# A stack of four modulated convolutions on one core: the last product in one piece, input transforms of the last quads in another order, and the last edge product seven turns later

## The chip, the core and the metric

The program runs on one core of a Trainium2 chip. The time is the device time of one execution in microseconds (us), and the span is the part of it from the first to the last profiled instruction. The engines are TensorE (PE, with its weight loads as PEld), VectorE (DVE), ScalarE (ACT), GpSimd (POOL) and SyncE (SP, which here only issues transfers). Each has its own queue of instructions and takes them strictly in order.

## The reference

The input `x` is 128 samples of 64 channels by 1024 points. Four layers of three taps are applied, and the result is added to `x`:

```python
def _layer(x, style, w, b, mw, mb, typ):
    s = style @ mw.T + mb
    weight = SCALE * w * s[:, None, :, None]
    demod = lax.rsqrt(jnp.sum(weight * weight, axis=(2, 3)) + EPS)
    weight = weight * demod[:, :, None, None]
    # 'same': 3 taps; 'upsample': transposed, step 2, then blur;
    # 'downsample': blur, then 3 taps with step 2
    ...
for i, typ in enumerate(('same', 'upsample', 'same', 'downsample')):
    out = _layer(out, style, weights[i], biases[i], mod_w[i], mod_b[i], typ)
x = x + out
```

Each sample has its own weights, since `style` differs per sample. All is float32.

## The kernel before, in words

The four layers are linear in `x` once the weights of a sample are known. So the kernel multiplies the four weight sets of a sample together, with the blurs, into one filter of nine taps (`Wf`), the residual being one more addend, and then runs this filter over `x`. The three outer points at either end of a row do not obey that filter; a separate small chain of products computes corrections for them.

Four samples make a **quad**: two lie on the two halves of the 128 partitions, and two stand side by side (index `c` or `s`, 0 and 1). There are 32 quads (`NQ`), numbered 0 to 31, and each is loaded as three planes of 344 columns (every third point).

The nine taps over three planes are done with five products instead of nine, each of three taps. Their inputs are sums and differences of planes made ahead: `T3` (`in3`), `G` (`in_g01`, `in_g2`), then from `G` the tiles `T12` (`in1`, `in2`, mostly on GpSimd) and `T04` (`in04`, on VectorE). `in04(q, pairs)` can be done for both pairs of samples at once or for one pair (`PAIR[0]`, `PAIR[1]`). There is one `G` buffer, and there are two `T04` buffers. The products are `conv3`, `conv1`, `conv2`, `conv4`, `conv0`: `conv4` and `conv0` read `T04`, `conv4` into the PSUM tile `Y`, the others into the quad's own pair of banks `psA`. Between products VectorE and ScalarE take intermediate sums (`copy_m3`, `sum1`, `sum2`), since the banks go on accumulating. `sum2` writes into `Y` what `conv4` then adds to.

The main loop is a software pipeline in an order written out by hand (no scheduler reorders it): `turn_of(q)` finishes quad q, runs the first products of quad n = q+1, makes the filter of quad c = q+2 and begins that of quad q+4. Turns 4 to 28 are such turns; after them comes a hand-written stretch for q = 29 and one for quads 30 and 31.

What the steps of the prediction touch:

- `product`, L807, issues the 12 matmuls of one product (each counts twice in the profile). In the last stretch the last product (`conv0` of quad 31) is made in two rounds: first the outer 88 columns at either side (`SIDES`), then the 166 in the middle (`MIDDLE`); after each, ScalarE turns bank 0 and VectorE bank 1 into the plane of `o` (`output`, L891), and each piece has its own store, on the ScalarE and the SyncE queue. `o` is one tile `o1` for both rounds.
- `SLOTS`, L1303: at the top of turn q, if q-1 is a key, one group of edge products is put on TensorE into the banks of quad q-1. The last group is `ends3`; `rest3` then reads it into the table of corrections `Oe`.
- `gather(q)` brings the edge points of quad q into `Oc`: for quads below `LATER_ENDS` as plain copies on ScalarE, for the later ones as a subtraction of `Oe` on GpSimd, one turn later. `correct_all` subtracts `Oe` from all the copies at once on VectorE and stores them; the rest are stored at the very end (`store_ends`).

Of the kernel before, what the change touches and what calls it, by code (L numbers as in the profile page):

```python
# [55 lines left out]
K = 3  # L56
# [7 lines left out]
def kernel(  # L64
# [9 lines left out]
    nc = tc.nc  # L74
    NP, P, NXC = x.shape
    B = 2 * NP
    NQ = B // 4
# [5 lines left out]
    nc_v, nc_a, nc_g = nc.vector, nc.scalar, nc.gpsimd  # L83
# [91 lines left out]
    NB = 342  # L175
    Y = ps_y.tile([P, 2, 512], F32, name="Y")
# [428 lines left out]
    def tap(kind, g):  # L605
        return range(9)[TAPS[kind]][g]
# [132 lines left out]
    Ts = {}  # L739
# [3 lines left out]
    BOTH_PAIRS = slice(0, 2)  # L743
    PAIR = slice(0, 1), slice(1, 2)
# [43 lines left out]
    def in04(q, pairs=BOTH_PAIRS):  # L788
        if q < NQ:
            t, g = t_tile(q, "T04"), Gs[q]  # L790
            a, b = g[:, pairs, :NJ], g[:, pairs, 2 * PL : 2 * PL + NJ]
            both = lambda v, step: bass.AP(
                v.tensor, v.offset, [*(list(d) for d in v.ap[:-1]), [step, 2], [1, NJ]]
            )
            nc_v.tensor_sub(t[:, pairs, :, :NJ], both(a, PL), both(b, 1))  # L795

    WHOLE = slice(0, NB)
    SIDES, MIDDLE = 88, slice(88, NB - 88)

    def columns(v, at):  # L800

        if at != SIDES:
            return v[..., at]
        ap = [list(d) for d in v.ap]
        return bass.AP(v.tensor, v.offset, [*ap[:-1], [ap[-1][0] * (NB - SIDES), 2], [ap[-1][0], SIDES]])

    def product(q, m, ps, groups=range(K), alone=False, at=WHOLE):  # L807

        W, H_ = Wq[q]
        tag, i = SLOT[m]  # L810
        for g in groups:
            for s, rows in enumerate(HALF):
                for c, cols in enumerate(HALF):
                    if m in (0, 4):
                        w = W[rows, tap(m // 2, g), c, :]
                    else:
                        w = H_[rows, m - 1, g, c, :]
                    nc.tensor.matmul(  # L818
                        columns(ps[s][cols], at),
                        w,  # L820
                        columns(Ts[q, tag][rows, c, i, g:], at),
                        start=(g == 0 and (m == 3 or alone)),
                        stop=(g == K - 1),
                        skip_group_check=True,
                    )
# [4 lines left out]
    m3c, y1w = {}, {}  # L830
# [7 lines left out]
    def banks(q):  # L838
        return A[q] if isinstance(A[q], list) else [A[q][:, s] for s in range(2)]
# [31 lines left out]
    def sum2(q, steps=(0, 1)):  # L871
        if 0 in steps:
            m3 = m3c.pop(q)
            for s, a in enumerate(banks(q)):
                sum_of(Y[:, s, :NB], m3[:, s], 3.0, a[:, :NB])
        for s, a in parts(q) if 1 in steps else ():
            nc_v.tensor_sub(y1w[q][:, s], y1w[q][:, s], a)

    def conv4(q, *groups):
        product(q, 4, Y_banks, groups or range(K))  # L880

    def conv0(q, *groups):
        product(q, 0, banks(q), groups)

    NO = NB + 2
    o_tiles = [const.tile([P, 2, K, NO], F32, name=f"o{i}") for i in range(2)]
    for t in o_tiles:
        nc_g.memset(t[:, :, :, NB:], 0.0)
    os = [t[:, :, :, :NB] for t in o_tiles] * (NQ // 2)

    def output(q, i, s, eng=nc_a, at=WHOLE):  # L891

        d3, add = td[:, q, s : s + 1], tb[:, q, s : s + 1]
        src = columns((banks(q)[s], y1w[q][:, s], Y[:, s])[i], at)
        dst = columns(os[q][:, s, i], at)
        if eng is nc_a:
            nc_a.activation(dst, src, AF.Identity, bias=add, scale=d3)  # L897
        else:
            eng.tensor_scalar(dst, src, d3, add, op0=ALU.mult, op1=ALU.add)  # L899

    def store(q, s, planes=slice(0, K), queue=nc.sync):
        queue.dma_start(
            out[q, :, s, planes.start * NO : planes.stop * NO],
            o_tiles[q % 2][:, s, planes].rearrange("c i j -> c (i j)"),
        )
# [262 lines left out]
    def edges(q, planes):  # L1168
        o = os[q].rearrange("c r i j -> c r j i")
        at, step = ((0, NB - 1), (0, NB - 2))[planes.start > 0]  # L1170
        return o[:, :, at : step + 1 : step, planes], 2 * q

    LATER_ENDS = NQ - 6

    def correct(q, planes, eng=nc_g):
        src, b = edges(q, planes)
        at = slice(b, b + 2)
        if eng is nc_a:
            eng.copy(Oc[:, at, :, planes], src)
        else:  # L1180
            eng.tensor_sub(Oc[:, at, :, planes], src, Oe[:, at, :, planes])  # L1181

    def gather(q):
        for planes in (slice(1, K), slice(0, 1)):
            correct(q, planes, nc_a if q < LATER_ENDS else nc_g)

    def correct_all(n):
        nc_v.tensor_sub(Oc[:, : 2 * n], Oc[:, : 2 * n], Oe[:, : 2 * n])
        store_ends(0, n)

    def store_ends(i, j, queue=nc.sync):
        at = slice(12 * i, 12 * j)
        queue.dma_start(out_ends[:, at], Oc.rearrange("c b e j -> c (b e j)")[:, at])
# [5 lines left out]
    BOTH = nc_a, nc_v  # L1199
# [100 lines left out]


    REST = PART[2]
    SLOTS = {9: (ends0, rest0), 10: (ends1, rest1), 12: (ends2, rest2), 16: (ends3, rest3)}  # L1303

    def high(n):
        return Y[:, 1, NB + 4 : NB + 4 + n]
# [44 lines left out]
    def last_factors():  # L1351
# [22 lines left out]
        14: lambda: (blur_side(0, 0), blur_side(1, 0)),  # L1374
        15: lambda: (blur_side(0, 1), blur_side(1, 1)),
        16: lambda: (blur_side(0, 2), blur_side(1, 2)),
        NQ - 5: lambda: correct_all(LATER_ENDS),
    }

    def extra(*at):  # L1380
# [2 lines left out]
    def side(work, q):  # L1383
        work.get(q, lambda: None)()
# [118 lines left out]
    def turn_of(q):  # L1503
        n, c, s = q + 1, q + 2, q + 4
        entry = q == FIRST
        stage2(c)
        if entry:
            sum2(q)
            conv4(q)
            combine_a(n)  # L1510
            r_sums(c, nc_v)
        else:
            if q - 1 in SLOTS:
                SLOTS[q - 1][0](banks(q - 1))
            conv2(q)
            r_sums(c, nc_g)
            if q - 1 in SLOTS:
                SLOTS[q - 1][1](A[q - 1])
            sum2(q)
            in2(n, nc_g)  # L1520
        side(TABLES, q)
        for i in range(3):
            load(c + 1, slice(i, i + 1))
        stage3_b(c, open_a(n))
        if entry:
            conv0(q, 0, 1)
        else:
            combine_a(n)
            conv4(q)
        stage3_a(c)  # L1530
        combine_b(n)
        conv3(n)
        if entry:
            copy_m3(n)
            stage1_a(s)
        outputs(q, 2)
        if not entry:
            if s < NQ:
                stage1_a(s)
            copy_m3(n)  # L1540
        in04(n)
        if sharing(q):
            share_sums(c + 1)
        in_g2(c)
        side(SIDE, q)
        if q in SMALL:
            l, bs = SMALL[q]
            nc_v.memset(high(bs.stop - bs.start), 0.0)
        conv0(q, *((2,) if entry else range(K)))
        if entry:  # L1550
            conv1(n, 0, 1)
        outputs(q, 1)
        if s < NQ:
            stage1_b(s)
        in_g01(c)
        if sharing(q):
            share(c + 1, banks(q))
            share_copy(c + 1)
        outputs(q, 0)
        if q < LATER_ENDS:  # L1560
            gather(q)
        conv1(n, *((2,) if entry else range(K)))
        if q in SMALL:
            small(q)
        sum1(n)
        in3(c)
        if q > LATER_ENDS:
            gather(q - 1)
        if s == NQ:
            in04(c, PAIR[0])  # L1570
        in1(c, nc_g)
        if s + 1 < NQ:
            scale3(s + 1)
# [6 lines left out]
    q, n, c = NQ - 3, NQ - 2, NQ - 1  # L1580
# [10 lines left out]
    outputs(q, 2)  # L1591
    copy_m3(n)
    in3(c)
    in04(n, PAIR[1])
    in_g01(c)
    stage3(c, 1)
    conv0(q, 0)
# [18 lines left out]
    q, n = NQ - 2, NQ - 1  # L1616
# [44 lines left out]
        plus(i, o[:, i, 2], Y_banks, one_td, m3[:, i])  # L1661
        store(q, i, slice(2, K))
    correct(q, slice(1, K), nc_v)
    for at in (SIDES, MIDDLE):
        product(q, 0, banks(q), at=at)
        for i, (eng, queue) in enumerate(zip(BOTH, (nc_a, nc.sync))):
            output(q, 0, i, eng, at)
            queue.dma_start(
                columns(out[q, :, i, :NO], at), columns(o_tiles[q % 2][:, i, 0], at)
            )  # L1670
        if at == SIDES:
            correct(q, slice(0, 1), nc_v)
            store_ends(LATER_ENDS, NQ)


# [74 lines left out]
```

## Time and profile before

| what | value |
|---|---|
| median of three runs | 477.81 us (477.81, 476.05, 477.82) |
| the profiled execution | 474.59 us |
| its span | 472.8 us |
| TensorE busy | 466.1 us, 99% of the span |
| VectorE, ScalarE, GpSimd busy | 414.7, 318.7, 176.8 us |
| mean granted TensorE clock | 0.999 |
| written to and read from memory | 34.01 and 35.03 MB, 146 GB/s over the span |

A busy TensorE is not one at its peak: matmuls are pipelined and their ends are modelled. A row of the timeline has start, duration, engine, line, operation, output and inputs, count, and in brackets how long the engine had been idle and who released it. `T` in it is `T3`, `T12` or `T04`, by the line: L764 is `in3`, L781 `in1`, L786 `in2`, L795 `in04`. L715 is a helper of many sums.

### The profile page before, as it was taken

Reading aid. Unit: us, or ns where it says so; the run is one execution under the profiler, and the core shown is the slowest. Engines: PE = TensorE matmul, PEld = TensorE weight load, DVE = VectorE, ACT = ScalarE, POOL = GpSimd, SP = SyncE. Lnnn points to the kernel's source line nnn. Section 1 sums busy time; section 2 is a strip of 40 time slices with the busy share of each in tenths; the row PEclk is TensorE's granted clock in tenths of the full one; section 3 lists DMA queues with packets and bytes.
Section 4 is the critical chain, followed back from the end, with each engine's and each line's share of the span. In section 5 each row is a group of like instructions: output and inputs, shape, how many; then the busy total and the mean of one; then the engine's idle time right before and its main releaser. Section 6 shows DMA issues by size and latency. Waiting matters only on the chain. (4 is left out here: it accounts for less than half of the span.)

```text
span 472.8 us, 27015 instructions
## 1 busy us (share of the span) xinstructions
PE 466.1 (99%) x12052; PEld 341.6 (72%) x12052; DVE 414.7 (88%) x678; ACT 318.7 (67%) x764; POOL 176.8 (37%) x216
## 2 busy tenths in 40 slices
PE   9999999999999999999999999999999999999995
PEld 8887778777767777767876677776677777777753
DVE  5899989778989999998899988889888888998994
ACT  5566676677766667765777757777766777776463
POOL 3634141763448542233332234432233442333310
PEclk9999999999999999999999999999999999999999
DMA  6326554554445553444544445544455554445224
GB/s 179 94 93 209 170 153 153 153 166 141 150 139 167 154 181 113 144 143 155 167 147 144 150 151 158 183 143 146 140 153 162 175 175 132 151 148 170 92 84 162
DMA packets 53380, 70.79 MB, mean 150 GB/s; under 512 B 6672, under 2 KB 51472, under 8 KB 53264
## 3 DMA queue, kind: packets, MB, share of 16 engines
q1 hardware_dynamic: 52768, 68.84, 46.0%
q8 instruction: 94, 1.54, 1.4%
q10 hardware_dynamic: 496, 0.22, 0.2%
q14 instruction: 22, 0.18, 0.1%
HBM read 35.03 MB, written 34.01 MB: 146 GB/s over the span
## 5 line engine op out<-in xcount | busy, mean ns | idle before, releaser
L818 PE MATMUL psA<-T,H 64*64 64x342 f32 x2304 | 186.4, 449 | 0.1
L818 PEld LDWEIGHTS psA<-T,H 64*64 64x64 f32 x2304 | 86.7, 133 | 49.8 <-issue 2.1
L715 DVE SCALAR_TENSOR_TENSOR G<-X 128x1378 f32<-128x1378 f32 (+2 forms) x65 | 78.3, 1210 | 0.3
L487 POOL TENSOR_TENSOR S<-S 128x128 f32<-128x128 f32 x28 | 21.4, 766 | 139.3 <-ACT S L402 139.1
L781 POOL TENSOR_TENSOR T<-G 128x688 f32<-128x688 f32 x28 | 46.5, 1660 | 71.3 <-DVE G L715 60.7
L818 PE MATMUL psA<-T,Wf 64*64 64x342 f32 (+2 forms) x792 | 64.4, 439 | 0.6 <-ACT o L897 0.4
L818 PE MATMUL Y<-T,Wf 64*64 64x342 f32 x768 | 62.9, 454 | 0.0
L402 ACT ACTIVATE psW<-psA 128x128 f32<-128x128 f32 x100 | 19.3, 268 | 54.0 <-PE psA L624 49.8
L402 ACT ACTIVATE R<-psR,tC 128x448 f32<-128x448 f32 x63 | 36.6, 631 | 28.3 <-PE psR L509 14.2
L715 DVE SCALAR_TENSOR_TENSOR Y<-m,psA 128x342 f32<-128x342 f32 x62 | 32.2, 519 | 26.4 <-PE psA L818 25.3
L795 DVE TENSOR_TENSOR T<-G 128x1376 f32<-128x1376 f32 (+1 forms) x34 | 52.7, 1551 | 0.0
L402 ACT ACTIVATE Wf<-psW,t 128x256 f32<-128x256 f32 (+2 forms) x76 | 32.7, 480 | 27.8 <-PE psW L624 27.6
L764 DVE TENSOR_TENSOR T<-X 128x688 f32<-128x688 f32 x32 | 50.6, 1581 | 0.0
L786 POOL TENSOR_TENSOR T<-G 128x688 f32<-128x688 f32 x28 | 47.2, 1687 | 0.0
L509 PE MATMUL psR<-S,E 64*64 64x64 f32 (+1 forms) x1472 | 46.4, 238 | 0.0
L431 PEld LDWEIGHTS psS<-wd,w2n 64*64 64x64 f32 x1120 | 33.9, 133 | 13.8
L509 PEld LDWEIGHTS psR<-S,E 64*64 64x64 f32 x1472 | 38.5, 134 | 5.4 <-ACT psR L532 0.2
L818 PEld LDWEIGHTS Y<-T,Wf 64*64 64x64 f32 x768 | 28.6, 132 | 19.0 <-DVE Y L715 0.2
L897 ACT ACTIVATE o<-psA,tb,td 128x342 f32<-128x342 f32 (+1 forms) x64 | 37.6, 646 | 6.8 <-PE psA L818 4.2
L818 PEld LDWEIGHTS psA<-T,Wf 64*64 64x64 f32 x792 | 29.4, 133 | 16.2 <-ACT o L897 0.7
L897 ACT ACTIVATE o<-y,tb,td 128x342 f32<-128x342 f32 x62 | 38.6, 681 | 0.4 <-issue 0.4
L897 ACT ACTIVATE o<-Y,tb,td 128x342 f32<-128x342 f32 x62 | 36.2, 642 | 3.0 <-PE Y L818 2.0
(186 smaller groups left out, 833.7 us busy)
## 6 DMA issues: line engine op xcount, KB each, us to landing
out<-o SPq DMA_DIRECT2D x190, 172.0 KB, 2.1
X<-in_x SPq DMA_DIRECT2D x150, 172.0 KB, 3.2
X<-in_x SPq DMA_DIRECT2D x14, 516.0 KB, 4.9
par<-in_params SPq DMA_DIRECT2D x3, 192.0 KB, 4.0
Xe<-in_x_ends SPq DMA_DIRECT2D x1, 192.0 KB, 2.8
par<-in_params SPq DMA_DIRECT2D x1, 160.0 KB, 2.6
out<-Oc SPq DMA_DIRECT2D x1, 156.0 KB, 1.8
par_s<-in_params_s SPq DMA_DIRECT2D x1, 120.0 KB, 3.0
```

The source lines that it names most:

```text
L402: nc_a.activation(dst, src, AF.Copy, scale=f)
L431: nc.tensor.matmul(ps[r][cols, at * C : (at + n) * C], weight[rows], wd[c if r == 0 else 1 - c][rows, taps], start=first, stop=last, skip_ ...
L487: nc_g.tensor_add(t[:, :, 2], t[:, :, 2], t[:, :, 0])
L509: nc.tensor.matmul(dst[r][cols], weight[rows], st[c if r == 0 else 1 - c][rows, slots, :], start=False, stop=last, skip_group_check=True,)
L715: nc_v.scalar_tensor_tensor(out, x, f, y, op0=ALU.mult, op1=op)
L764: nc_v.tensor_sub(t[:, pairs, 0, :NJ], plane(X, 3, pairs), plane(X, 1, pairs))
L781: eng.tensor_add(t[:, :, 0, :NJ], plane(g, 2), plane(g, 1))
L786: eng.tensor_sub(t[:, :, 1, :NJ], plane(g, 2), plane(g, 1))
L795: nc_v.tensor_sub(t[:, pairs, :, :NJ], both(a, PL), both(b, 1))
L818: nc.tensor.matmul(columns(ps[s][cols], at), w, columns(Ts[q, tag][rows, c, i, g:], at), start=(g == 0 and (m == 3 or alone)), stop=(g == ...
L897: nc_a.activation(dst, src, AF.Identity, bias=add, scale=d3)
```

## The change

The two-round form of the last product is removed, with its helper for columns. `conv0` of quad 31 is issued whole, each bank is read out whole, and each of the two samples has one store of its plane 0. The edge points of plane 0 and their store come after both.

`T04` of quad 29: pair 0 is made at the end of turn 27, pair 1 in the middle of turn 28 (both were made in the middle of turn 28). `T04` of quad 30: both pairs are made at the end of turn 28 (before: pair 0 there, pair 1 in the stretch for q = 29).

`ends3` and `rest3` move from the top of turn 17 to the top of turn 24. `LATER_ENDS` falls from 26 to 25, and `correct_all` moves from turn 27 to turn 26, for 25 quads and not 26; the points of quad 25 are gathered by GpSimd in turn 26 instead of by ScalarE in turn 25.

```diff
-    def product(q, m, ps, groups=range(K), alone=False, at=WHOLE):
+    def product(q, m, ps, groups=range(K), alone=False):
...
-                        columns(ps[s][cols], at),
+                        ps[s][cols, :NB],
                         w,
-                        columns(Ts[q, tag][rows, c, i, g:], at),
+                        Ts[q, tag][rows, c, i, g : g + NB],
...
-    LATER_ENDS = NQ - 6
+    LATER_ENDS = NQ - 7
...
-    SLOTS = {9: (ends0, rest0), 10: (ends1, rest1), 12: (ends2, rest2), 16: (ends3, rest3)}
+    SLOTS = {9: (ends0, rest0), 10: (ends1, rest1), 12: (ends2, rest2), 23: (ends3, rest3)}
...
-        NQ - 5: lambda: correct_all(LATER_ENDS),
+        NQ - 6: lambda: correct_all(LATER_ENDS),
...
-        in04(n)
+        in04(n, PAIR[1] if s == NQ else BOTH_PAIRS)
...
+        if s == NQ - 1:
+            in04(c, PAIR[0])
         if s == NQ:
-            in04(c, PAIR[0])
+            in04(c)
         in1(c, nc_g)
...
     in3(c)
-    in04(n, PAIR[1])
     in_g01(c)
...
-    for at in (SIDES, MIDDLE):
-        product(q, 0, banks(q), at=at)
-        for i, (eng, queue) in enumerate(zip(BOTH, (nc_a, nc.sync))):
-            output(q, 0, i, eng, at)
-            queue.dma_start(
-                columns(out[q, :, i, :NO], at), columns(o_tiles[q % 2][:, i, 0], at)
-            )
-        if at == SIDES:
-            correct(q, slice(0, 1), nc_v)
-            store_ends(LATER_ENDS, NQ)
+    conv0(q, *range(K))
+    for i, (eng, queue) in enumerate(zip(BOTH, (nc_a, nc.sync))):
+        output(q, 0, i, eng)
+        store(q, i, slice(0, 1), queue)
+    correct(q, slice(0, 1), nc_v)
+    store_ends(LATER_ENDS, NQ)
```

Two places show how the instructions stand. The first is VectorE from the middle of turn 28 to the sum that `conv4` of quad 29 waits for (`Y`). `T04_29` and `T04_30` are the tiles of quads 29 and 30; 1376 columns are both pairs, 688 one. Before:

```order
L795 TENSOR_TENSOR T04_29_8422<-G29_8174 128x1376
L715 SCALAR_TENSOR_TENSOR G30_8424<-X0_102 128x2x344
L715 SCALAR_TENSOR_TENSOR G30_8424<-X0_102 128x2x689
L715 SCALAR_TENSOR_TENSOR y1_29_8459<-psA29_8328,m3_29_8420 128x684
L764 TENSOR_TENSOR T3_30_8461<-X0_102 128x688
L795 TENSOR_TENSOR T04_30_8465<-G30_8424 128x688
L715 SCALAR_TENSOR_TENSOR Y_118<-m3_29_8420,psA29_8328 128x342 x2
```

And after the change, the same stretch of the same engine:

```order
L795 TENSOR_TENSOR T04_29_8244<-G29_8176 128x688
L715 SCALAR_TENSOR_TENSOR G30_8425<-X0_102 128x2x344
L715 SCALAR_TENSOR_TENSOR G30_8425<-X0_102 128x2x689
L715 SCALAR_TENSOR_TENSOR y1_29_8460<-psA29_8330,m3_29_8422 128x684
L764 TENSOR_TENSOR T3_30_8462<-X0_102 128x688
L795 TENSOR_TENSOR T04_30_8466<-G30_8425 128x1376
L715 SCALAR_TENSOR_TENSOR Y_118<-m3_29_8422,psA29_8330 128x342 x2
```

Half of `T04_29` has left the head of the stretch, and `T04_30` has become whole right ahead of the sum into `Y`. The missing half of `T04_29` now stands one turn earlier, between `T3_29` and the sum into `Y` of quad 28.

The second place is the end of the VectorE queue, from the sum of plane 1 of quad 31 on. Before:

```order
L1627 SCALAR_TENSOR_TENSOR o1_141<-psA31_1_8680,times_722,y1_31_8697 128x342
L1658 TENSOR_TENSOR m3_31_8693<-m3_31_8693,m1_31_8696 128x684
L1627 SCALAR_TENSOR_TENSOR o1_141<-Y_118,td_136,m3_31_8693 128x342 x2
L1181 TENSOR_TENSOR Oc_172<-o1_141,Oe_171 128x4x2
L899 TENSOR_SCALAR o1_141<-psA31_1_8680,td_136,tb_137 128x2x88
L1181 TENSOR_TENSOR Oc_172<-o1_141,Oe_171 128x4
L899 TENSOR_SCALAR o1_141<-psA31_1_8680,td_136,tb_137 128x166
```

After the change:

```order
L1618 SCALAR_TENSOR_TENSOR o1_141<-psA31_1_8680,times_722,y1_31_8697 128x342
L1649 TENSOR_TENSOR m3_31_8693<-m3_31_8693,m1_31_8696 128x684
L1618 SCALAR_TENSOR_TENSOR o1_141<-Y_118,td_136,m3_31_8693 128x342 x2
L1171 TENSOR_TENSOR Oc_172<-o1_141,Oe_171 128x4x2
L889 TENSOR_SCALAR o1_141<-psA31_1_8680,td_136,tb_137 128x342
L1171 TENSOR_TENSOR Oc_172<-o1_141,Oe_171 128x4
```

Two pieces of bank 1 have become one, and the edge points of plane 0 come behind all of it.

The SyncE queue ends with four stores of planes, a piece, the edge points and a piece before:

```order
L902 DMA out_0<-o0_140 128x344 x6
L902 DMA out_0<-o1_141 128x344 x4
L1668 DMA out_0<-o1_141 128x2x88
L1193 DMA out_1<-Oc_172 128x72
L1668 DMA out_0<-o1_141 128x166
```

After the change it ends with these:

```order
L892 DMA out_0<-o0_140 128x344 x6
L892 DMA out_0<-o1_141 128x344 x6
L892 DMA out_0<-o0_140 128x344 x6
L892 DMA out_0<-o1_141 128x344 x5
L1183 DMA out_1<-Oc_172 128x84
```

The last transfer issued is now that of the edge points, 84 columns for seven quads where it was 72 for six.

More of the change, by code (lines that the diff above doesn't have):

```diff
@@ L795, in in04 @@
             nc_v.tensor_sub(t[:, pairs, :, :NJ], both(a, PL), both(b, 1))
[L797 to L805, printed above, removed]
-    def product(q, m, ps, groups=range(K), alone=False, at=WHOLE):
+    def product(q, m, ps, groups=range(K), alone=False):
         W, H_ = Wq[q]
@@ L889, with output @@
     os = [t[:, :, :, :NB] for t in o_tiles] * (NQ // 2)
-    def output(q, i, s, eng=nc_a, at=WHOLE):
+    def output(q, i, s, eng=nc_a):
         d3, add = td[:, q, s : s + 1], tb[:, q, s : s + 1]
-        src = columns((banks(q)[s], y1w[q][:, s], Y[:, s])[i], at)
-        dst = columns(os[q][:, s, i], at)
+        src = (banks(q)[s][:, :NB], y1w[q][:, s], Y[:, s, :NB])[i]
+        dst = os[q][:, s, i]
         if eng is nc_a:
```

## Prediction, made before the changed kernel ran

> **What bounds the kernel now.** I read the page first, for who is busy.
>
> ```profile
> PE 466.1 (99%) x12052; PEld 341.6 (72%) x12052; DVE 414.7 (88%) x678; ACT 318.7 (67%) x764; POOL 176.8 (37%) x216
> ```
>
> TensorE has work nearly all the time, so an edit counts only where it takes work from TensorE, opens a gap in it, or touches the end of the run, where TensorE has nothing left. I then cut the span into stretches of one turn each (from one copy of `m3` to the next). Each row has the stretch, its length, and the busy time of each engine.
>
> ```profile
> 268.27:283.42 15.15, 15.15 (x424) 10.98 (x420) 13.71 (x23) 10.12 (x26) 4.80 (x4) 1.00 0.46 144
> 366.81:380.71 13.90, 13.90 (x392) 9.81 (x388) 12.11 (x19) 10.04 (x27) 4.81 (x4) 1.00 0.48 154
> 408.50:422.40 13.90, 13.90 (x392) 10.46 (x388) 12.11 (x19) 9.80 (x24) 4.80 (x4) 1.00 0.51 157
> 422.40:435.13 12.73, 12.73 (x360) 9.47 (x356) 11.57 (x18) 8.04 (x20) 6.07 (x8) 1.00 0.52 165
> ```
>
> A plain turn is 13.90 us at full clock; the one with `ends3` is 15.15. VectorE has 13.90 - 12.11 = 1.79 us to spare per turn. The last of these rows is turn 27's end and turn 28's start, shorter because no new filter is begun.
>
> Then the end of the run, from the timeline of each engine, and the page's chain of waits (its last pieces).
>
> ```profile
> 462.76 2.16 PE L818 MATMUL Y<-T,Wf 64*64 64x342 f32 x24
> 464.48 1.33 PE L818 MATMUL psA<-T,Wf 64*64 64x176 f32 x24
> 465.62 0.50 ACT L897 ACTIVATE o<-psA,tb,td 128x176 f32<-128x176 f32 x1 [1.39 <-PE psA L818]
> 466.44 0.46 DVE L899 TENSOR_SCALAR o<-psA,td,tb 128x176 f32<-128x176 f32 x1
> 466.93 0.39 SPq L1668 DMA_DIRECT2D out<-o  x1
> 466.96 1.06 PE L818 MATMUL psA<-T,Wf 64*64 64x166 f32 x20 [0.29 <-DVE o L899]
> 467.42 0.44 SPq L1193 DMA_DIRECT2D out<-Oc  x1
> 468.76 0.49 ACT L897 ACTIVATE o<-psA,tb,td 128x166 f32<-128x166 f32 x1 [2.64 <-DMA out<-o]
> 469.69 0.45 DVE L899 TENSOR_SCALAR o<-psA,td,tb 128x166 f32<-128x166 f32 x1 [2.51 <-DMA out<-o]
> 470.16 0.33 SPq L1668 DMA_DIRECT2D out<-o  x1
> ...
> 466.93 2.63 DMA out<-o
> ```
>
> The middle round's product is through at 466.96 + 1.06 = 468.02, yet its two readouts begin at 468.76 and 469.69: each waits 2.5 to 2.6 us for the landing of the side round's store, because both rounds write one tile `o1` and the second is held as if it overwrote what the first store still reads. VectorE's wait is the chain: product, readout, store (2.63), readout, store, end.
>
> **The end, worked out.** One product of 24 wide matmuls takes 2.16 us (the row at 462.76). It can start where the first round did, so bank 1 is ready at 464.48 + 2.16 = 466.64, and VectorE, free before that (its piece at 466.44 came after everything else), starts at about 466.7. A readout of 342 columns on VectorE isn't in the trace: 166 take 0.45 and 176 take 0.46, a slope of 0.001 per column, which makes 0.63; a sum of the same width from PSUM takes half of the first row here, 0.53.
>
> ```profile
> 465.27 1.06 DVE L1627 SCALAR_TENSOR_TENSOR o<-Y,td,m 128x342 f32<-128x342 f32 x2
> 467.01 0.17 DVE L1181 TENSOR_TENSOR Oc<-o,Oe 128x4 f32<-128x4 f32 x1
> ```
>
> I take 0.6 for the readout, so 467.3, and SyncE issues the store at 467.33. The edge points (0.17 by the second row, plus a gap of 0.1) are done at 467.57, and their store is issued when SyncE is free of the one ahead: 0.49 passed between these two issues before (466.93 to 467.42) with an issue of 0.39, now one of 0.33, so 0.43, at 467.76. How long a store takes to land:
>
> ```profile
> out<-o SPq DMA_DIRECT2D x190, 172.0 KB, 2.1
> out<-Oc SPq DMA_DIRECT2D x1, 156.0 KB, 1.8
> out<-o SPq DMA_DIRECT2D x1, 83.0 KB, 1.7
> out<-Oc SPq DMA_DIRECT2D x1, 36.0 KB, 2.3
> DMA to landing us min/median/max: 1.7/2.1/5.9
> ```
>
> The plane's store lands at 467.33 + 2.1 = 469.4. That of the edge points (84 columns, 42 KB) lands after 1.8 to 2.3; I take 2.0, between, since the 2.3 shared the engines with two stores in small pieces, which are gone. It lands at 469.8 and is last. Before, the last landed at 470.16 + 1.7 = 471.86 and the span ended 0.9 later at 472.8; so now at 470.7. **Gain at the end: 2.1**, between 1.8 (landing in 2.3) and 2.5 (the plane's store last, readout at 0.53).
> The page "DMA: Bandwidth & Descriptors" of the Trainium skill (section "Anatomy of one DMA — SWDGE (gpsimd) path") gives, for transfers issued from GpSimd, 2.0 us plus the bytes at 436 GB/s; as an estimate from it, 43 KB would take 2.1 and the gain be 2.0. These transfers are issued from SyncE, and 1.7 and 1.8 stand above, so here the fixed part is smaller than that.
>
> **The edge products.** `ends3` costs 15.15 - 13.90 = 1.25 us of TensorE in turn 17 and will cost the same in turn 24, which is a plain one in the second row. `rest3` (two sums) goes along, into a turn with 1.79 spare. Zero. `correct_all` takes 0.74:
>
> ```profile
> L1188 DVE TENSOR_TENSOR Oc<-Oc,Oe x1: 739/739/739, 423.0 to 423.0; 128x312 f32<-128x312 f32 x1
> 425.99 1.67 POOL L781 TENSOR_TENSOR T<-G 128x688 f32<-128x688 f32 x1 [2.02 <-DVE G L715]
> ```
>
> In turn 26 it finds the same 1.79 (third row), and leaves turn 27. Its store goes with it on SyncE's queue, past six stores and six loads, which all wait for their data there longer than for it. The two gathers of quad 25 go to GpSimd, ahead of `in1`, which in the next turn stood 2.02 idle behind the same two. If these covers failed, the 0.74 would be the price; I take zero.
>
> **T04.** Here is the stretch in which it moves, VectorE unless marked.
>
> ```profile
> 426.61 1.78 DVE L764 TENSOR_TENSOR T<-X 128x688 f32<-128x688 f32 x1
> 429.41 1.07 DVE L715 SCALAR_TENSOR_TENSOR Y<-m,psA 128x342 f32<-128x342 f32 x2 [1.02 <-PE psA L818]
> 434.28 1.58 DVE L795 TENSOR_TENSOR T<-G 128x1376 f32<-128x1376 f32 x1
> 435.95 2.38 DVE L715 SCALAR_TENSOR_TENSOR G<-X 128x688 f32<-128x688 f32 x2
> 438.50 1.65 POOL L781 TENSOR_TENSOR T<-G 128x688 f32<-128x688 f32 x1 [6.52 <-PE psA L818]
> 438.58 0.87 DVE L715 SCALAR_TENSOR_TENSOR y<-psA,m 128x684 f32<-128x684 f32 x1 [0.24 <-PE psA L818]
> 439.37 1.52 DVE L764 TENSOR_TENSOR T<-X 128x688 f32<-128x688 f32 x1
> 440.11 2.29 POOL L786 TENSOR_TENSOR T<-G 128x688 f32<-128x688 f32 x1
> 440.81 2.32 DVE L795 TENSOR_TENSOR T<-G 128x688 f32<-128x688 f32 x1
> 443.05 1.06 DVE L715 SCALAR_TENSOR_TENSOR Y<-m,psA 128x342 f32<-128x342 f32 x2
> 444.17 1.36 PEld L818 LDWEIGHTS Y<-T,Wf 64*64 64x64 f32 x24 [0.22 <-DVE Y L715]
> 448.69 0.87 DVE L795 TENSOR_TENSOR T<-G 128x688 f32<-128x688 f32 x1
> ...
> 449.00 1.90 PE L818 MATMUL psA<-T,H 64*64 64x342 f32 x24
> ...
> 451.16 0.86 DVE L715 SCALAR_TENSOR_TENSOR y<-psA,m 128x684 f32<-128x684 f32 x1
> 452.14 3.11 PEld L818 LDWEIGHTS psA<-T,H 64*64 64x64 f32 x48 [0.68 <-issue]
> ```
>
> One half costs 0.87 alone (448.69), the whole 1.58. Where GpSimd works on `T12` at the same time, one waits for the other: the half at 440.81 took 2.32 and ended 0.73 after GpSimd's instruction (442.40), which itself took 2.29 where it takes 1.65 alone.
>
> Turn 27: the new half of `T04_29` comes after the row at 426.61, which ends at 428.39, and ahead of the sum at 429.41, which had 1.02 idle waiting for TensorE. 428.3 + 0.87 = 429.2: hidden, with 0.2 to spare, and 0.74 more since `correct_all` has left this turn.
>
> Turn 28: the half left gives VectorE 1.58 - 0.87 = 0.71 sooner. `G` of quad 30 ends at 437.6 and not at 435.95 + 2.38 = 438.33, so GpSimd's `in1`, which began 0.17 behind it, starts at 437.8 and ends at 439.4; the sum at 438.58 waits for TensorE and stays. `T3_30` (0.87 alone) and GpSimd's `in2` (1.65) then take turns from 439.4 on; whichever is first, both are done by 441.7 to 441.8, and the whole `T04_30` behind them ends by 443.2 to 443.3 instead of 443.13. The sum into `Y`, which TensorE already waits for, is 0.1 late. Without the head start of GpSimd it would be 0.71 late (1.58 for 0.87 after the same wait), so the price lies between 0 and 0.71; I take 0.1, since what released `in1` one turn earlier was `G` (425.99), although the row at 438.50 names TensorE.
>
> The stretch for q = 29 loses the half at 448.69. The next sum (451.16) was due when TensorE had finished `conv1`, at about 450.95 (449.00 + 1.90, from the modelled ends), so 0.2 of its start were VectorE's fault, and the wait at 452.14, which hangs on that sum, gives them back. Net **zero**, between +0.7 lost and 0.2 won.
>
> **Sum.** 472.8 - 2.1 = 470.7, so 472.5 for the profiled execution (474.59, of which 1.8 lies outside the span). The three runs lie 1.5 to 3.2 above it; against their median, 477.81 - 2.1 = **475.7**, or 0.44% less. A change under 0.5%, 2.4 us, is about what a measurement of this kernel can't tell from none.
>
> **Rivals.** *The port wait eats part of it.* `T04_30` whole meets GpSimd's `in2` and conv4 of quad 29 starts 0.7 late, nothing given back: gain 1.4, 476.4. For it: the 2.32. Against: the earlier `G`.
> By "SBUF — State Buffer" of the Trainium skill (section "Who interferes with whom"), a VectorE instruction with two SBUF inputs and a GpSimd one that reads SBUF exclude each other for a whole instruction, whoever issues first; the rows at 440.11 and 440.81 agree. A change that adds 0.71 of such work next to GpSimd's is then exposed to the full length of `in2`, which is this rival.
>
> *More than the sum.* VectorE's lead in the stretch for q = 29 closes the whole wait of 0.68 at 452.14, and the edge store lands in 1.8, which makes 2.3: gain 3.0, 474.8. Against: after 452 every VectorE step waits for TensorE in turn, so a lead is not carried.
>
> *Slower.* The last store is a small one behind another; a store took up to 5.9 to land. Then 467.76 + 5.9 + 0.9 = 474.6, 1.8 later than before: 479.6. It decides from a landing of 4.1. Against: no loads are left by then to share the engines with.
>
> *Nothing gained*, if the readouts waited for something else than the store recorded: 477.8. Against: the product was done at 468.02, and both idled until a store landed.
>
> **Chances.** Forecast 0.55; port wait 0.15; more 0.2; slower 0.05; nothing 0.05. The forecast lies 0.3 from the bound of faster, so a fifth of it may be measured there, and most of "more": faster 0.28; slower 0.06; same 0.66. The range takes 474.8 and 476.4 and half of the runs' own spread of 1.77 on either side, rounded outward: 473.8 to 477.4.
>
> **What would show it.** No readout waiting for a store at the end, one product of 342 columns from about 464.5, the edge store issued near 467.8 and last, a span near 470.7; turn 24 at 15.15 and turn 17 at 13.90; `T04_30` at 440.2 to 441.7 taking 1.6 to 3.0, and the sum into `Y` within 0.2 of 443.05. Wrong would be a `Y` late by over 0.5, or a last store that lands over 2.5 after its issue.

## The result and the profile after

The changed kernel takes 474.93 us, the median of seven runs (474.52 to 476.0), beside 477.75 for seven runs of the kernel before. The two medians are 2.8 us apart. The ratio that is worked out from all of these runs is 0.9949, with a 95% interval of 0.9928 to 0.9970, so 2.4 us less, between 1.4 and 3.4. The prediction was 475.7 us.

The first row of the page shows nearly the same instructions, and 24 matmul records fewer, which is the second round of the last product.

```profile
PE 467.9 (99%) x12028; PEld 345.4 (73%) x12028; DVE 413.2 (87%) x677; ACT 318.1 (67%) x761; POOL 176.4 (37%) x218
```

The profiled execution is no faster: its span is 474.2 us, and that of the kernel before 472.8. So one span against the other would have given the wrong sign, and the two have to be compared stretch by stretch. I cut both into four: to the first copy of `m3`, to that of quad 28, to the first matmul of the last product, and to the end. The columns are the stretch, its length, the busy time (and count) of PE, PEld, DVE, ACT and POOL, the granted clock, the DMA share and GB/s. Before:

```profile
0.00:21.08 21.08, 19.97 (x592) 18.23 (x596) 14.55 (x50) 11.21 (x27) 12.03 (x35) 1.00 0.43 122
21.08:422.40 401.32, 401.32 (x10596) 293.52 (x10592) 358.46 (x567) 281.11 (x684) 152.84 (x165) 1.00 0.49 154
422.40:464.48 42.08, 41.97 (x832) 27.91 (x828) 38.77 (x57) 25.40 (x52) 11.96 (x16) 1.00 0.38 127
464.48:472.77 8.29, 2.90 (x54) 1.95 (x46) 2.91 (x7) 0.99 (x2) 0.00 (x0) 0.95 0.41 132
```

And the changed kernel:

```profile
0.00:22.95 22.95, 21.08 (x592) 18.96 (x596) 14.39 (x50) 11.23 (x28) 11.95 (x35) 1.00 0.41 117
22.95:425.97 403.02, 402.51 (x10596) 295.04 (x10592) 358.54 (x568) 280.84 (x682) 153.79 (x167) 1.00 0.49 153
425.97:468.15 42.18, 42.12 (x832) 30.33 (x828) 37.54 (x56) 25.41 (x52) 10.63 (x16) 1.00 0.37 123
468.15:474.21 6.06, 2.16 (x30) 1.07 (x22) 2.71 (x6) 0.64 (x1) 0.00 (x0) 1.00 0.52 181
```

The last row is the edit at the end: 8.29 to 6.06, **2.23 us less**. The third holds the moved `T04`: 42.08 to 42.18, 0.10 more. Together that is 2.13 less, inside the interval of the times. The other two rows, 1.87 and 1.70 longer, hide it in this execution. The first of them is the start-up, where the code is the same in both kernels. Here is a step of ScalarE that waits for one of the loads of parameters, in the timeline of before and then of the changed kernel:

```profile
6.73 0.62 ACT L1232 ACTIVATE wsq<-par 64x192 f32<-64x192 f32 x2 [0.30 <-DMA par<-in_params]
```

```profile
8.60 0.61 ACT L1222 ACTIVATE wsq<-par 64x192 f32<-64x192 f32 x2 [1.85 <-DMA par<-in_params]
```

In these two traces that load landed later by as much (8.60 - 6.73 = 1.87) as the whole stretch is longer. It doesn't explain every trace: in the run of the edge products alone the same step starts at 6.93, and the stretch is still the longest of all, 23.36; what delays that one was not found. Over the ten traces of this study the first copy of `m3` starts between 21.08 and 23.36 us, and 21.08 is the kernel before: its profiled execution began luckier than any other, which is part of why it lay 3.2 below its own median.

In the second row single turns are longer than their like. In the changed kernel the turn from 299.25 takes 14.25 and the next one, with the same instructions of TensorE, 13.90. Such turns stand at other places in other traces, and one turn that is long everywhere varies: it takes 15.70 in the kernel before (from 210.67), 15.95 in the changed kernel and 15.45 in the run of the edge products alone. What makes them was not found. Both stretches vary from run to run by more than the change is worth, while the last two repeat within 0.1 us wherever the code is the same. So the experiments are read by the last two.

| kernel | to first `m3` | to `m3` of quad 28 | to the last product | last product to end | median us | ratio to before (95%) |
|---|---|---|---|---|---|---|
| before | 21.08 | 401.32 | 42.08 | 8.29 | 477.75 | |
| changed | 22.95 | 403.02 | 42.18 | 6.06 | 474.93 | 0.9949 (0.9928 to 0.9970) |
| last product in one piece, alone | 22.40 | 401.84 | 42.07 | 6.05 | 474.15 | 0.9937 (0.9913 to 0.9960) |
| `T04` alone | 22.82 | 401.60 | 42.17 | 8.32 | 476.71 | 0.9999 (0.9980 to 1.0017) |
| edge products alone | 23.36 | 400.80 | 42.07 | 8.22 | 476.27 | 0.9988 (0.9969 to 1.0008) |
| middle piece in its own tile | 21.80 | 400.83 | 42.12 | 7.69 | 475.56 | 0.9975 (0.9957 to 0.9994) |
| changed, without the head start | 23.02 | 401.96 | 42.69 | 6.06 | 474.66 | 0.9965 (0.9945 to 0.9984) |
| two halves | 22.46 | 401.21 | 42.07 | 7.68 | 475.98 | 0.9979 (0.9960 to 0.9998) |
| one piece, edge store on ScalarE's queue | 22.27 | 400.80 | 42.07 | 6.06 | 474.34 | 0.9953 (0.9935 to 0.9971) |
| own tile and own range | 23.05 | 401.14 | 42.08 | 6.99 | 475.12 | 0.9966 (0.9949 to 0.9983) |

Each ratio of the last eight rows is against runs of the kernel before that were made with them on the same chip; their median was 476.74 for the first four of these rows and 476.55 for the other four. So rows are compared by their ratios and not by their medians. One of the twelve runs of the edge products alone took 984.06 us, twice as long as the others, and is left out of its row.

The end of the changed kernel, from the timeline (start, duration, engine, line, operation):

```profile
468.15 2.16 PE L808 MATMUL psA<-T,Wf 64*64 64x342 f32 x24
470.11 0.64 ACT L887 ACTIVATE o<-psA,tb,td 128x342 f32<-128x342 f32 x1 [2.22 <-PE psA L808]
470.36 0.63 DVE L889 TENSOR_SCALAR o<-psA,td,tb 128x342 f32<-128x342 f32 x1 [0.17 <-PE psA L808]
470.78 0.36 ACTq L892 DMA_DIRECT2D out<-o  x1
471.10 0.17 DVE L1171 TENSOR_TENSOR Oc<-o,Oe 128x4 f32<-128x4 f32 x1
471.46 0.39 SPq L1183 DMA_DIRECT2D out<-Oc  x1
```

Neither readout waits for a store now; both are released by TensorE. What remains is the product, one readout, the edge points and the last landings.

### The profile page after: what moved, and what is told of

The parts are those of the page before. It is cut to its first block, busy times and chain, and to the rows that moved or that the text cites. A ratio compares the mean times of both kernels' runs of the same rounds, so it can differ in the third digit from the quotient of the medians.

```text
span 474.2 us, 26959 instructions
## 1 busy us (share of the span) xinstructions
PE 467.9 (99%) x12028; PEld 345.4 (73%) x12028; DVE 413.2 (87%) x677; ACT 318.1 (67%) x761; POOL 176.4 (37%) x218
## 4 chain that ended last, share of the span: by engine, by line
PE 96%; DVE 1%; DMA 1%; SPq 0%; ACT 0%; issue 0%; DVEq 0%
PE psA L808 47%; PE Y L808 12%; PE psR L509 10%; PE psW L624 7%; PE psA L624 7%; PE psS L431 5%; PE psR L592 4%; PE psA L509 2%; DMA par<-in_params 1%; PE psA L1045 1%; DVE T L764 0%; DVE T L795 0%; PE Y L258 0%; DVE Y L715 0%; DVE y L715 0%
## 5 line engine op out<-in xcount | busy, mean ns | idle before, releaser
L808 PEld LDWEIGHTS psA<-T,H 64*64 64x64 f32 x2304 | 88.6, 133 | 48.1 <-issue 2.0
L808 PE MATMUL psA<-T,Wf 64*64 64x342 f32 x768 | 63.8, 448 | 0.0
L795 DVE TENSOR_TENSOR T<-G 128x1376 f32<-128x1376 f32 (+1 forms) x34 | 51.3, 1507 | 0.0
L887 ACT ACTIVATE o<-psA,tb,td 128x342 f32<-128x342 f32 x63 | 37.2, 651 | 5.0 <-PE psA L808 5.0
```

The source lines that it names most:

```text
L808: nc.tensor.matmul(ps[s][cols, :NB], w, Ts[q, tag][rows, c, i, g : g + NB], start=(g == 0 and (m == 3 or alone)), stop=(g == K - 1), skip_ ...
```

## The experiments

**Each part alone.** The first kernel is the one before with only the tail block exchanged:

```diff
-    for at in (SIDES, MIDDLE):
-        product(q, 0, banks(q), at=at)
...
-        if at == SIDES:
-            correct(q, slice(0, 1), nc_v)
-            store_ends(LATER_ENDS, NQ)
+    conv0(q, *range(K))
+    for i, (eng, queue) in enumerate(zip(BOTH, (nc_a, nc.sync))):
+        output(q, 0, i, eng)
+        store(q, i, slice(0, 1), queue)
+    correct(q, slice(0, 1), nc_v)
+    store_ends(LATER_ENDS, NQ)
```

> The kernel before with the last product in one piece alone. Theory (the end of the run carries all of the gain): from the start of the last product to the end of the span 6.0 to 6.1 us as in the changed kernel, instead of 8.3; the time falls by 2.2 us, a ratio of 0.9954. Rival (the other two parts bring the rest of the 2.8 us between the medians): the same 6.0 at the end, but other stretches as before, and a ratio near that of the end alone while T04 or the edge products alone gain 0.3 us or more each.

Its last stretch:

```profile
466.31:472.36 6.05, 2.16 (x30) 1.05 (x22) 2.71 (x6) 0.64 (x1) 0.00 (x0) 0.92 0.52 181
```

6.05 is the changed kernel's 6.06, and the ratio 0.9937 is, if anything, below the changed kernel's; their intervals overlap. The end carries the whole gain.

The second has only the three edits of `in04`:

```diff
-        in04(n)
+        in04(n, PAIR[1] if s == NQ else BOTH_PAIRS)
...
+        if s == NQ - 1:
+            in04(c, PAIR[0])
         if s == NQ:
-            in04(c, PAIR[0])
+            in04(c)
...
-    in04(n, PAIR[1])
```

> The kernel before with the changed order of T04 alone. Theory: the stretches from the copy of m3 of quad 28 to the start of the last product change by 0.1 us in sum at most, later at conv4 of quad 29 and given back at conv2 of quad 30; ratio 1.000 within 0.001. Rival (VectorE's lead is worth something): that sum is shorter by 0.5 us, ratio 0.999. Rival (the port wait): longer by 0.7, ratio 1.0015.

The stretch from the copy of quad 28 to the last product:

```profile
424.42:466.59 42.17, 42.14 (x832) 30.33 (x828) 38.07 (x57) 25.38 (x52) 10.87 (x16) 1.00 0.38 127
```

42.17, where the kernels without this edit have 42.07 to 42.12: it costs some 0.1, and the times show nothing of it (0.9999). Neither rival came: not 0.7 lost, not 0.5 won.

The third has only the move of `ends3`, `rest3` and `correct_all`:

```diff
-    LATER_ENDS = NQ - 6
+    LATER_ENDS = NQ - 7
...
-    ... 16: (ends3, rest3)}
+    ... 23: (ends3, rest3)}
...
-        NQ - 5: lambda: correct_all(LATER_ENDS),
+        NQ - 6: lambda: correct_all(LATER_ENDS),
```

> The kernel before with the last group of edge products in turn 24 and correct_all in turn 26 alone. Theory: turn 24 takes 15.15 us, turn 17 13.90, turns 26 and 27 13.90 each, sum zero; ratio 1.000 within 0.001. Rival: one of the turns 25 to 27 is longer by some tenths, since ScalarE's gather went to GpSimd and correct_all stands in a turn with a filter to make.

Its turns 17 and 24:

```profile
270.04:283.94 13.90, 13.90 (x392) 9.77 (x388) 13.08 (x21) 10.12 (x26) 4.80 (x4) 1.00 0.50 157
367.32:382.47 15.15, 15.15 (x424) 11.02 (x420) 12.73 (x21) 10.03 (x26) 4.80 (x4) 1.00 0.46 144
```

The 1.25 us have changed turns and nothing else has moved: the last two stretches (42.07 and 8.22 in the table) are those of before, and the three turns after turn 24 take 13.90, 13.89 and 13.90. The rival, a longer turn among 25 to 27, didn't come. The cost of this part is zero, as far as the trace can tell.

**What held the two rounds.** The prediction put the whole wait on the shared tile `o1`. This kernel is the one before, with the middle piece in a tile of its own, so that its readout can't touch what the first store reads:

```diff
+    o_mid = const.tile([P, 2, NB - 2 * SIDES], F32, name="o_mid")
...
-            output(q, 0, i, eng, at)
-            queue.dma_start(
-                columns(out[q, :, i, :NO], at), columns(o_tiles[q % 2][:, i, 0], at)
-            )
+            to = o_mid[:, i] if at == MIDDLE else columns(o_tiles[q % 2][:, i, 0], at)
+            output(q, 0, i, eng, at, to)
+            queue.dma_start(columns(out[q, :, i, :NO], at), to)
```

> The kernel before, still two rounds, but the middle round writes a tile of its own, which is stored from there. Theory (the second readouts waited for the first stores only because both rounds write one tile): no readout waits for a store; the middle product still waits some 0.3 us for the first readouts, ends at 3.6 us after the start of the last product, its VectorE readout at 4.1 and the last landing at 5.9, so 6.7 from the start of the last product to the end of the span instead of 8.3; the time falls by 1.6 us, ratio 0.9967. Rival (they waited for something else, such as the store's queue): 8.3 as before, ratio 1.000.

The readouts of the middle on ScalarE and VectorE, the issue of SyncE's second store, and the row of the waits of SyncE's queue that belongs to it (total, times, longest):

```profile
468.08 0.49 ACT L898 ACTIVATE o_mid<-psA,tb,td 128x166 f32<-128x166 f32 x1 [1.70 <-PE psA L818]
468.33 0.45 DVE L900 TENSOR_SCALAR o_mid<-psA,td,tb 128x166 f32<-128x166 f32 x1 [0.90 <-PE psA L818]
469.78 0.33 SPq L1670 DMA_DIRECT2D out<-o_mid  x1
```

```profile
SPq L1670 <- DMA out<-o: 1.6, 1, 1.6
```

Both readouts are free, as expected, and wait for TensorE alone. But the last stretch, from 464.75 on, is 7.69 and not 6.7. VectorE's piece is ready at 468.33 + 0.45 = 468.78, and its store is issued only at 469.78, 1.0 us later: SyncE's queue waits, 1.6 us in all, for the landing of the first store. The two outer pieces are written by one store, and in `out` they lie on either side of the middle; it is held as if it wrote over the first. There is a second hold behind the first, which the trace of before could not show.

Two halves have no such interleaving, neither in the tile nor in the output:

```diff
-    for at in (SIDES, MIDDLE):
+    for at in (slice(0, NB // 2), slice(NB // 2, NB)):
         product(q, 0, banks(q), at=at)
...
-        if at == SIDES:
-            correct(q, slice(0, 1), nc_v)
-            store_ends(LATER_ENDS, NQ)
+    correct(q, slice(0, 1), nc_v)
+    store_ends(LATER_ENDS, NQ)
```

> The kernel before, the last product still in two rounds, but of 171 columns side by side, so that their ranges in the banks, in o1 and in the output don't overlap; the edge points come after both. Theory (two rounds cost time only by the overlap of their ranges): no readout, no store and no matmul waits for the other round; last product's rounds follow each other without a gap, and from its start to the end of the span it is 6.0 us, within 0.2 of the one piece. Rival (two rounds cost in themselves, by more weight loads and stores): 6.6 or more.

```profile
465.74 1.30 PE L818 MATMUL psA<-T,Wf 64*64 64x171 f32 x24
467.39 0.51 PE L818 MATMUL psA<-T,Wf 64*64 64x171 f32 x4 [0.34 <-ACT o L897]
468.20 1.09 PE L818 MATMUL psA<-T,Wf 64*64 64x171 f32 x20 [0.30 <-DVE o L899]
469.08 0.49 ACT L897 ACTIVATE o<-psA,tb,td 128x171 f32<-128x171 f32 x1 [1.75 <-DMA out<-o]
469.34 0.45 DVE L899 TENSOR_SCALAR o<-psA,td,tb 128x171 f32<-128x171 f32 x1 [1.19 <-PE psA L818]
469.82 0.33 SPq L1668 DMA_DIRECT2D out<-o  x1
470.26 0.37 SPq L1193 DMA_DIRECT2D out<-Oc  x1
```

```profile
465.74:473.42 7.68, 2.90 (x54) 1.95 (x46) 2.90 (x7) 0.99 (x2) 0.00 (x0) 0.88 0.44 142
```

No store holds the second round now. SyncE's second store goes out at 469.82, 0.03 behind its readout (469.34 + 0.45 = 469.79). The row of ScalarE's second readout does name a store, but it starts 3.34 us after the product (469.08 - 465.74), and in the own-tile kernel, where TensorE released it, 3.33 (468.08 - 464.75): that store cost nothing.

And yet the end is at 7.68: the expectation of 6.0 fell, and its rival, 6.6 or more, came. TensorE's second round waits for both readouts of the first, 0.34 and 0.30, though it writes other columns of the banks. The product lasts from 465.74 to 468.20 + 1.09 = 469.29, or 3.55 us, where one piece takes 2.16. Of these 1.39 more, 0.64 are the two waits. The other 0.74 is TensorE itself: it is busy for 2.90 with 24 matmul records more, where one piece takes 2.16 (by the modelled ends). Part of that may still come from the interruptions, since the first 24 take 1.30 and the interrupted 24 of the second round 0.51 + 1.09 = 1.60. Two rounds like the first would be 2 x 1.30 - 2.16 = 0.44 longer than one piece, so two rounds cost TensorE some 0.4 to 0.7 in themselves, beside the waits in the banks. The readout is shorter by 0.63 - 0.45 = 0.18, so the last piece is read out 1.2 us later than with one piece.

The end is 7.68 - 6.06 = 1.62 later. Most of the remaining 0.4 is the landing: VectorE's second half landed 2.5 us after its issue, and its whole plane in the changed kernel 2.1; why is not known. Here the edge points also come after the second round, as in the changed kernel and unlike the kernel before. "PSUM — Partial Sum Buffer" of the Trainium skill (section "PSUM bank collisions raise a hardware error") says that the compiler adds a dependency between any two instructions of different engines on the same part of a bank, whichever columns they touch; the trace agrees, with the two waits above, though no run shows whether they are that dependency.

The last of this series keeps the sides and the middle, the middle's own tile, and stores the two sides by a store each (the lines of the middle's own tile are left out):

```diff
...
+            if at == SIDES:
+                for side in (slice(0, SIDES), slice(NB - SIDES, NB)):
+                    queue.dma_start(out[q, :, i, side], o_tiles[q % 2][:, i, 0, side])
+            else:
+                queue.dma_start(columns(out[q, :, i, :NO], at), to)
```

> Two rounds with the middle in a tile of its own, and the sides stored as two pieces each, so that no store's range in the output spans that of another. Theory (with the tile apart, the last store itself was held until the first store of the same sample had landed, since that one's range in the output spans the middle): the middle's store is issued on SyncE at about 4.1 us after the start of the last product instead of 5.0, and the span ends 6.7 after that start instead of 7.7. Rival (SyncE was held by its queue): 5.0 and 7.7 stay.

Readout and store of the middle on VectorE and SyncE, what the store waited for, and its landing (size, then us from issue):

```profile
469.85 0.45 DVE L900 TENSOR_SCALAR o_mid<-psA,td,tb 128x166 f32<-128x166 f32 x1 [0.90 <-PE psA L818]
470.32 0.33 SPq L1674 DMA_DIRECT2D out<-o_mid  x1
```

```profile
SPq L1674 <- DVE o_mid L900: 0.2, 1, 0.2
```

```profile
out<-o_mid SPq DMA_DIRECT2D x1, 83.0 KB, 1.9
```

```profile
466.26:473.25 6.99, 2.90 (x54) 1.95 (x46) 2.91 (x7) 0.99 (x2) 0.00 (x0) 0.98 0.48 156
```

The store goes right behind its readout, 470.32 - 466.26 = 4.06 us after the product's start; with the range shared it was 469.78 - 464.75 = 5.03. By the landings in the trace, SyncE's two side stores are in only at 5.03 and 5.22 on the same count, so the hold didn't merely end sooner: it is gone. So the range was the second hold. The end was expected at 6.7 and came at 6.99, 0.2 of that from a landing in 1.9 where 1.7 was taken. The series now splits the gain, in this order of removal: 8.29 to 7.69 for the tile (0.60), to 6.99 for the range in the output (0.70), and to 6.06 for the second round (0.93). The last part holds both the waits in the banks and TensorE's own extra time; no run takes them apart.

**What sets the end now.** One piece alone, with the edge store on ScalarE's queue instead of behind the plane's on SyncE's:

```diff
-    store_ends(LATER_ENDS, NQ)
+    store_ends(LATER_ENDS, NQ, nc_a)
```

> The last product in one piece alone (T04 and edge products as before), and the last store of edge points issued by ScalarE instead of SyncE, where it stood behind the store of bank 1. Theory: issued 0.15 us sooner, and 5.9 us from the start of the last product to the end of the span instead of 6.05; with T04 as before 42.07 and not 42.18 to that start; in all 0.25 us less than the changed kernel, too little for the times to tell. Rival (the end is set by the landing of bank 1's store, not by the edge store): 6.05.

```profile
468.33 0.34 ACTq L1193 DMA_DIRECT2D out<-Oc  x1
```

```profile
out<-Oc ACTq DMA_DIRECT2D x1, 36.0 KB, 2.0
```

The last product starts at 465.14 here. The store is issued 468.33 - 465.14 = 3.19 us after that, 0.12 earlier than the changed kernel's 471.46 - 468.15 = 3.31, and the end stays at 6.06: it took that much longer to land. By the landings in the trace, the plane of bank 1 is in at 5.00 and the edge points at 5.17 here, and at 4.99 and 5.16 in the changed kernel. The small store lands 0.17 behind the large one, whichever queue issued it, so the theory of 5.9 fell, and the rival fits: the plane of bank 1 sets the end. In all ten traces the last edge store was issued 0.32 to 0.54 after SyncE's store of a plane or piece ahead of it, and landed 0.16 to 0.28 behind it. "DMA: Bandwidth & Descriptors" of the Trainium skill (section "Queues, rings and completion order") says that a completion is posted only after every earlier write of the same DMA engine, across its queues; the landings agree, though only one of these runs moved the edge store to another queue.

**The head start of GpSimd.** The changed kernel with the whole `T04` of quad 29 back in the middle of turn 28:

```diff
-        in04(n, PAIR[1] if s == NQ else BOTH_PAIRS)
+        in04(n)
...
-        if s == NQ - 1:
-            in04(c, PAIR[0])
```

> The changed kernel, but T04 of quad 29 stays whole in the middle of turn 28, so that VectorE (and with it GpSimd's in1) has no head start, while T04 of quad 30 is still whole at the end of turn 28. Theory (the head start is what keeps the price of the whole T04 small): conv4 of quad 29 starts 8.3 us after conv1 of quad 29 instead of 7.63 before and 7.80 in the changed kernel; some 0.1 to 0.2 of it is given back at conv2 of quad 30; from the copy of m3 of quad 28 to the start of the last product 42.6 us instead of 42.07 before and 42.18 changed. Rival (the order of GpSimd and VectorE on the port sets the price, not the head start): 7.8 as in the changed kernel, and 42.2.

`conv1` of quad 29, the two instructions that read SBUF together, and `conv4`:

```profile
439.25 2.00 PE L808 MATMUL psA<-T,H 64*64 64x342 f32 x24
442.69 2.28 POOL L786 TENSOR_TENSOR T<-G 128x688 f32<-128x688 f32 x1
443.38 3.04 DVE L795 TENSOR_TENSOR T<-G 128x1376 f32<-128x1376 f32 x1
447.46 1.96 PE L808 MATMUL Y<-T,Wf 64*64 64x342 f32 x24 [0.47 <-DVE Y L715]
```

`conv1` to `conv4` takes 447.46 - 439.25 = 8.21 us, expected 8.3, and the stretch to the last product 42.69, expected 42.6. So the half moved to turn 27 is worth 0.51 us: without it, the whole `T04` of quad 30 meets GpSimd's instruction, takes 3.04 where it takes 1.58 undisturbed, and TensorE waits. That is the mechanism of the prediction's rival, brought about by this edit. The loss is read from the trace: the ratios, 0.9965 here and 0.9949 for the changed kernel, have intervals that overlap.

## Why the prediction was right, point by point

**The end.** Forecast 2.1, between 1.8 and 2.5; measured 2.23, and 2.24 by itself. The terms, counted from the last product's start: VectorE starts at +2.21 (470.36 - 468.15; forecast +2.2); its readout of 342 columns takes 0.63 (taken at 0.6); the edge store is issued at +3.31 (forecast 467.76 - 464.48 = +3.28); and it lands after

```profile
out<-Oc SPq DMA_DIRECT2D x1, 42.0 KB, 1.9
```

1.9, where 2.0 was taken. The 0.1 by which the gain exceeds the forecast is this landing. One part of the mechanism was off here: the prediction let the edge store set the end by its own issue and landing, and by the run with ScalarE's queue its issue doesn't matter; it comes in 0.17 behind the plane. The forecast came out all the same, since the two landings were forecast 0.4 apart and lay 0.17 apart.

What the prediction had wrong is the reason for the size, not the size. It named one hold, on the tile, and that one gives only 0.60 when it alone is removed. Behind it stood a second, on the range in the output, and under both the second round itself, with its waits in the banks and TensorE's extra time. The sum came out since it was made from the new order of events, from the product's start to the last landing, and one piece leaves no second piece for any of these to act on, known or not. That is a merit of the change and not of the diagnosis. The own-tile kernel was costed in the same way, event by event, and missed by 1.0 (6.7 expected, 7.69 measured), because there an unseen hold was left. The waits in the banks stood in the trace of before, 0.29 of TensorE's time released by VectorE's readout, and were read past.

**The edge products.** Zero forecast, zero measured: turn 24 of the changed kernel is

```profile
271.26:285.17 13.91, 13.91 (x392) 9.78 (x388) 13.09 (x21) 10.13 (x27) 4.80 (x4) 1.00 0.51 157
369.09:384.26 15.17, 15.17 (x424) 10.88 (x420) 12.74 (x21) 10.05 (x27) 4.81 (x4) 1.00 0.47 144
```

the second row, and turn 17 the first. The two sums of `rest3` and the 0.74 of `correct_all` found their cover.

**T04.** Here the timeline of turn 27 and then of the stretch up to `conv4` of quad 29, in the changed kernel:

```profile
431.87 0.86 DVE L795 TENSOR_TENSOR T<-G 128x688 f32<-128x688 f32 x1
432.98 1.07 DVE L715 SCALAR_TENSOR_TENSOR Y<-m,psA 128x342 f32<-128x342 f32 x2 [0.25 <-PE psA L808]
...
441.42 1.66 POOL L781 TENSOR_TENSOR T<-G 128x688 f32<-128x688 f32 x1 [5.81 <-DVE G L715]
443.02 1.66 POOL L786 TENSOR_TENSOR T<-G 128x688 f32<-128x688 f32 x1
443.05 2.36 DVE L764 TENSOR_TENSOR T<-X 128x688 f32<-128x688 f32 x1
445.33 1.58 DVE L795 TENSOR_TENSOR T<-G 128x1376 f32<-128x1376 f32 x1
446.84 1.06 DVE L715 SCALAR_TENSOR_TENSOR Y<-m,psA 128x342 f32<-128x342 f32 x2
447.95 1.36 PEld L808 LDWEIGHTS Y<-T,Wf 64*64 64x64 f32 x24 [0.29 <-DVE Y L715]
```

In turn 27 the half is hidden, with 0.25 us left ahead of the sum (forecast 0.2). In turn 28 GpSimd's `in1` is released by `G`, as the prediction claimed against the name in the row of before. `in2` came first this time and `T3` waited for it (2.36), then the whole `T04` ran undisturbed (1.58): the other order of the two that the prediction allowed, with the same end. The times forecast, 441.7 to 441.8 for both and 443.2 to 443.3 for `T04`, are not the sums of the times alone that stand beside them (439.4 + 0.87 + 1.65 = 441.9, and 1.58 more is 443.5). Counted from the start of `conv1` they came out nonetheless: shifted by 440.15 - 436.54 = 3.61, `T3` ends at 441.8 and `T04` at 443.3. An instruction that waited ended less than its own time alone behind the other (`T3` 0.73 behind `in2`). From the start of `conv1` to that of `conv4`, and from there to `conv2` of the next quad, before and then after:

```profile
436.54:444.17 7.63, 7.63 (x173) 5.66 (x165) 7.35 (x8) 2.68 (x5) 3.89 (x2) 1.00 0.30 101
444.17:452.17 8.00, 7.89 (x123) 4.37 (x121) 7.81 (x13) 4.79 (x10) 0.74 (x1) 1.00 0.23 79
```

```profile
440.15:447.95 7.80, 7.75 (x173) 6.97 (x165) 6.75 (x7) 2.80 (x6) 3.26 (x2) 1.00 0.30 100
447.95:455.84 7.89, 7.89 (x120) 4.36 (x121) 7.02 (x12) 4.66 (x9) 0.21 (x1) 1.00 0.26 90
```

0.17 is lost (0.1 was forecast) and 0.11 given back (0.2 was). The net of zero is in truth 0.10 over the whole stretch. The rival of the port wait was real as a mechanism, and the run without the head start shows that the head start kept it away.

**Against the median.** 475.7 was the median shown less 2.1; the runs gave 474.93 beside a median of 477.75. The gap of 0.8 between forecast and result is within the spread of these runs, 474.52 to 476.0: the medians of the kernel before alone were 477.81, 477.75, 476.74 and 476.55 in four sets of runs, the first of them part of the second. Whether the true gain is 2.1 or 2.4 these times can't tell, and the two last stretches of the traces say 2.13. The span of 470.7 that was to show it did not come (474.2): it was reckoned from the one execution with the luckiest start. The range was rounded by more than was said: half of 1.77 on either side of 474.8 and 476.4 gives 473.9 to 477.3, and the time measured lies in that as well.

## What to carry to other kernels

Splitting the last step of a program so that its stores begin sooner can be held up by whatever the pieces share: here the tile (0.60 us), the spanned range of the output (0.70), and the banks, which together with the second round's own extra time on TensorE cost 0.93. One hid behind another, so taking away the wait that the trace names gave only a quarter of the gain. No split that shares nothing was run. To cost a removal, lay out the new order of events from its start to the last landing, and don't subtract the wait; where something shared is left, as in the own-tile kernel, even that can miss a hold that the trace doesn't show yet. And where start-up alone varies by 2.3 us, compare traces by stretches and not by spans.

## What the runs showed of the hardware

- A store of two outer pieces held what was done with the middle between them until it had landed, both in the tile that it reads (readouts idle for 2.5 to 2.6 us) and in the memory that it writes (the next store's queue waited 1.6 us, 1.0 of it with the piece ready). With a tile of its own for the middle the first wait is gone, and with one store for each side the second. Whether the hold is the hardware's or in the waits that the program was built with, these runs don't tell.
- At the end of these programs a store of one run of columns per row, 36 to 172 KB, landed in 1.7 to 2.5 us, with no order by size. The store of two separate runs per row (88 KB) took 2.4 to 2.6, and one of its sides alone (44 KB) 1.8 to 2.7.
- The small last store, issued 0.32 to 0.54 us after a larger one, landed 0.16 to 0.28 behind it in ten traces, in one of them from another queue.
- Nearly the same program's first 21 to 23 us vary by 2.3 us between executions. Between the kernel before and the changed one a load that landed 1.87 later accounts for it; in general the cause is open.
